# A four-layer graph network on one Trainium2 core: zero-filled operands, projections read together, halves with banks of their own, and some one-hot rows built by ScalarE

## The chip, the cores and the metric

The kernel runs on one core of a Trainium2 chip. The core has a matrix engine (TensorE, PE in the profile, with its weight loads as PEld), a vector engine (VectorE, DVE), an activation engine (ScalarE, ACT), a general engine (GpSimd, POOL) and a queue engine (SyncE, SP). Data lies in SBUF with 128 partitions; TensorE writes to PSUM, which has eight banks of 128 x 512 fp32 each. The metric is device time in microseconds for one launch.

## The reference

There are 32 graphs (batches) of 512 nodes with 128 features and a 0/1 adjacency matrix. Each of four layers normalizes x, clips it at zero, computes an update and adds it to x.

```python
h = jnp.maximum(_layernorm(x, axis=-1), 0.0)
x = x + _L0_gnn_ref(h, adj, L0_gnn_W, L0_gnn_b)   # max over neighbours of relu(p_i + q_j + b)
h = jnp.maximum(_layernorm(x, axis=-1), 0.0)
x = x + _L1_gnn_ref(h, adj, ...)                  # four dense layers over both directions of adj
h = jnp.maximum(_layernorm(x, axis=-1), 0.0)
x = x + _L2_gnn_ref(h, adj, L2_gnn_weight, L2_gnn_bias)   # row-normalized adj @ (h @ W) + b
h = jnp.maximum(_layernorm(x, axis=-1), 0.0)
x = x + _L3_gnn_ref(h, adj, nodemask, ...)        # four rounds of message and GRU cell
...
# layer 0
p = jnp.einsum('bnd,do->bno', x, W1 - W2)
q = jnp.einsum('bnd,do->bno', x, W2)
pre = p[:, :, None, :] + q[:, None, :, :] + b
h = jax.nn.relu(pre) * adj[..., None]
return jnp.max(h, axis=2)
# one of the four layers inside layer 1
src_agg = jnp.einsum('bjv,bij->biv', src, _l2norm(adj, 2))
dst_agg = jnp.einsum('bjv,bji->biv', dst, _l2norm(adj, 1))
upd = jnp.concatenate([src_agg, self_rep, dst_agg], axis=2)
return jnp.tanh(upd @ wu + bu)
# one of the four rounds of layer 3
m = jnp.einsum('bjn,bjd->bnd', adj, hw)
h = _gru_cell(m, h, w_ih[i], w_hh[i], b_ih[i], b_hh[i])
```

## The kernel before

A batch of 512 nodes is handled as NT = 4 tiles of 128 nodes. The function `batch` chains four stages for one batch.

`prepare` normalizes x, makes the adjacency matrix and its transpose (`at`) in SBUF, computes q and p of layer 0 by TensorE (`pq`), and writes the table of q to DRAM. It counts, by a triangular matmul (`pc`), which neighbour in its half block of 64 nodes each neighbour is; ScalarE copies the counts to `cc`, and SyncE copies these to both halves of the partitions (`ccd`). It forms keys by matmul (`pkey`), takes the eight largest by VectorE (`top`) for the neighbours beyond four in a half block, and transposes a small table of degree factors `sc` (`psc`).

`gathers` computes the maximum over neighbours. For each source block jt and each slot k from 1 to 4, VectorE compares `ccd` with 64 + k, which gives one-hot rows `oh` of 128 x 1024. Two matmuls with the split values of q (`qhl`) pick the q of the k-th neighbour (`pa`), and VectorE keeps the running maximum in `acc`. Up to seven leftover neighbours are fetched by indirect DMA on GpSimd's queue into `G` and joined into `gm`.

`layer1` runs four dense layers. A layer transposes its input (`pf`), splits it into a high part (ScalarE) and a low part (VectorE), and multiplies both by `at` and by `an`, sixteen matmuls into two banks `pg`, with VectorE scaling each bank into `ag`. It then sums in the bank `pu`: a bias matmul of `b8` with `rows` (8 partitions deep), and the products of the earlier features and of `ag` with fused weights. ScalarE takes the tanh of the bank. `layer23` does layer 2 (one aggregate, four 128-column projections `po`, each added to x by VectorE) and the four GRU rounds of layer 3 (`pk`, `pg3`, `phn`, `pxn`, `ph`). In the last batch alone the GRU rounds run by halves of 256 nodes; both halves of `ph` lie in one bank, and so do the two products `phn` and `pxn` of a half.

Nothing of this is issued in the order in which it is written. Every call is noted in a `Flow` (line 285), which issues all instructions by a list scheduler: it holds up to AHEAD = 6 batches open, estimates each instruction's cost, and gives the engine that can start first the waiting instruction with the earliest due time. A due time is a batch's place times PACE less the length of what follows less a lead that depends on the stage (`LEADS`). `FIRST`, `LAST` and `WEIGHTS` shift the places of the first and last batches and of the weight preparation. `BANKS` says how many PSUM banks each of four users is guaranteed: ps0 (prepare), ps1 (layer 1), ps2 (layers 2 and 3) and ps3 (the `pa`); the rest of the eight is shared. The scheduler knows a dependency only through the view that an instruction names: `mm` and `tr` take a view of the bank that they write, and `mm` may name the whole bank instead by `group`. Where TensorE would stand idle for long, the scheduler inserts idle-time matmuls (`spin`).

```python
F.mm(po[:, t, :], mT[:, t, :], W.w2, start=True, stop=True)
F.mm(flat(pu), W.b8[:, i, :], rows, start=True, stop=False)
F.vec.tensor_scalar(oh, ccd[jt], NBASE + k, None, ALU.is_equal)
op.due = n * self.pace - op.due - op.lead
```

All recorded instructions carry line 510, where the scheduler issues them, so the profile is read by tile names. Weights are prepared in `FastWeights` (`first`, `rest`, `last`) in the same flow.

Of the kernel before, what the change touches and what calls it, by code (L numbers as in the profile page):

```python
# [32 lines left out]
CODES = ((0, 1), (P, 1), (2 * P, 2), (4 * P, 4))  # L33
NLEFT = 7
PACE = 45.35
SPACING = 1.8
AHEAD = 6
BANKS = (2, 1, 2, 1)

LEADS = {  # L40
    "prepare": -33.2, "counts": -28.6, "keys": -38.2, "rows": -9.6,
    "gather0": 12.6, "gather1": -3.5, "gather2": -1.7, "gather3": -10.5,
    "first": 14.4, "layer1": -15.5, "layer10": -39.2, "layer11": -39.2,
    "layer12": -26.1, "layer13": -57.9, "layer2": 50.7, "layer3": 187.5,
    "layer30": 155.2, "layer31": 193.8, "layer32": 81.5, "layer33": 66.2,
    "out": 33.8,
}
FIRST = (-0.01, -0.0, -0.31, 0.0)
LAST = (0.0, -0.23, -0.17, -0.97, -0.05)
WEIGHTS = (-5.87, -1.69, -2.33)  # L50
# [205 lines left out]
class Engine:  # L256
# [5 lines left out]
    def __getattr__(self, op):  # L262
        fn = getattr(self.real, op)

        def note(*args, **kw):
# [12 lines left out]
            fast = self.name == "vec" and op == "tensor_scalar" and outs[0].free_size() > 256  # L278
# [6 lines left out]
class Flow:  # L285
# [50 lines left out]
    def cost(self, engine, op, outs, ins):  # L336
# [4 lines left out]
        if "dma" in op:  # L341
            if engine != "pool":
                width = 2 if outs[0].dtype == BF16 else 4
                return 0.48 if engine == "sync" else 0.42, 2.0 + outs[0].size() * width / 1.2e5
            return (1.25, 6.0) if "indirect" in op else (0.7, 4.0)
# [52 lines left out]
    def mm(self, out, lhsT, rhs, start, stop, group=None):  # L398

        n = rhs.free_size()  # L400
# [9 lines left out]
    def tr(self, out, in_, ident):  # L410
        self.note(
            "pe", self.nc.tensor.transpose, (out, in_, ident), {}, [out], [in_, ident],
            0.109 if in_.dtype == F32 else 0.056, 0.16,
        )
# [189 lines left out]
class FastWeights:  # L604
# [5 lines left out]
    def __init__(self, nc, F, a, const, mid, ps):  # L610
# [47 lines left out]
        nc.gpsimd.memset(self.sign[0:4, 1:2], 0.0)  # L658
        self.nc, self.a, self.const, self.n = nc, a, const, n

    def own(self, shape, dtype, name):
        return self.F.tile(self.const, shape, dtype, name, name)

# [28 lines left out]
    def rest(self):  # L692
# [31 lines left out]
        self.b8 = self.own([8, NL1, P], F32R, "b8r")  # L724
# [6 lines left out]
        for i in range(NL1):  # L731
# [4 lines left out]
            for k, nm in enumerate(("ws", "wn", "wd")):  # L736
# [8 lines left out]
                F.vec.tensor_copy(wt, pt[:, 0:ch, :])  # L745
# [10 lines left out]
            for k in range(2):  # L756
# [11 lines left out]
                self.b8[:, i, :], hi.bitcast(F32), self.sign[0:8, 0:1], full, ALU.mult, ALU.add  # L768
            )

    def last(self):
# [14 lines left out]
        F.vec.tensor_copy(w3t, pt[:, 0:NL3, :])  # L786
        self.gh, self.gm = [], []
        for l in range(NL3):
            for nm, dst in (("hh", self.gh), ("ih", self.gm)):
# [9 lines left out]
                if nm == "hh":  # L799
                    F.vec.tensor_copy(t, pg[:, 0:3, :])  # L800
                else:
                    gt = self.temp("xn2", f"gt_{l}")[:, 0:3, :]
                    F.vec.tensor_copy(gt, pg[:, 0:3, :])
# [19 lines left out]
def fast(ctx: ExitStack, tc: tile.TileContext, a: dict, out: bass.AP, bad):  # L823
# [12 lines left out]
    F.share(ps, 8, {f"ps{s}": n for s, n in enumerate(BANKS)} | {"idle": 0})  # L836

# [58 lines left out]
    def transposed(s, src, name):  # L896

        pt = pst(s, name)
        for t in range(NT):
            F.tr(pt[:, t, :], src[:, t, :], W.ident)  # L900
        return pt
# [9 lines left out]
    def parts(s, src, tag, buf=plain, cuts=(slice(None),)):  # L911
# [3 lines left out]
        for c in cuts:  # L915
            v, h, l = ((w if len(cuts) == 1 else w[:, c, :]) for w in (src, hi, lo))
            F.act.copy(h, v)
            F.vec.tensor_sub(l, v, h.bitcast(F32))
        return hi, lo

    def aggregate(s, two, m, name):

        pg = pst(s, name)
        hi, lo = two
        for jt in range(NT):
            F.mm(flat(pg), hi[:, jt, :], m[:, jt, :], start=(jt == 0), stop=False)
            F.mm(flat(pg), lo[:, jt, :], m[:, jt, :], start=False, stop=(jt == NT - 1))
# [3 lines left out]
    def prepare(b, xt, af):  # L931
# [64 lines left out]
        F.lead = LEADS["counts"]  # L996
# [16 lines left out]
        F.lead = LEADS["keys"]  # L1013
# [4 lines left out]
        sc = F.tile(small, [P, 6, NT], F32, tag="sc", name=f"sc_{b}", bufs=4)  # L1018
# [36 lines left out]
        F.tr(pt[0 : 6 * NT, 0, :], sc.rearrange("p k t -> p (k t)"), W.ident)  # L1055
# [7 lines left out]
    def gathers(b, at, ccd, qhl, pn, tab, idx, has, dinv):  # L1063
# [15 lines left out]
        for jt in range(NT):  # L1079
            F.lead = LEADS[f"gather{jt}"]  # L1080
            for k in range(1, KSLOT + 1):
                oh = F.tile(big, [P, 2, N], F32R, tag="oh", name=f"oh_{b}_{jt}_{k}", bufs=3)
                F.vec.tensor_scalar(oh, ccd[jt], NBASE + k, None, ALU.is_equal)
# [7 lines left out]
        F.lead = LEADS["first"]  # L1091
# [16 lines left out]
    def layer1(b, x1, an, at, dinv):  # L1108
# [6 lines left out]
        rows = F.tile(mid, [8, N], F32R, tag="rows", name=f"rows_{b}")  # L1115
# [3 lines left out]
        F.act.copy(rows, row8)  # L1119
# [3 lines left out]
        feat = {"h": hT}  # L1123
        agg = {}
        new = "h"
        for i in range(NL1):
            F.lead = LEADS[f"layer1{i}"]
            names = INPUTS[i]
            w = W.w1[i]
            if i:  # L1130

                pt = transposed(1, feat[new], f"pf_{b}_{i}")
                two = parts(1, pt, f"{b}_1_{i}")
            ag = F.tile(mid, [P, 2, N], F32, tag="ag" + {"f2": "f1"}.get(new, new), name=f"ag_{b}_{i}")
            for k, m in ((0, at), (1, an)):
                pg = aggregate(1, two, m, f"pg_{b}_{i}_{k}")
                F.vec.tensor_mul(ag[:, k, :], flat(pg), rbc[:, k, :])
            agg[new] = ag
            pu = pst(1, f"pu_{b}_{i}")
            F.mm(flat(pu), W.b8[:, i, :], rows, start=True, stop=False)  # L1140
            late = []
            for c, nm in enumerate(names):
                F.mm(flat(pu), w[:, 1, c, :], flat(feat[nm]), start=False, stop=False)
                for k in range(2):
                    if nm == new:
                        late.append((c, k))
                        continue
                    F.mm(flat(pu), w[:, 2 * k, c, :], agg[nm][:, k, :], start=False, stop=False)
            for c, k in late:
                F.mm(flat(pu), w[:, 2 * k, c, :], ag[:, k, :], start=False, stop=(k == 1))  # L1150
# [3 lines left out]
            F.act.activation(fi, pu, AF.Tanh, bias=W.bu[:, i : i + 1])  # L1154
            feat[new] = fi
        F.lead = LEADS["layer2"]
# [613 lines left out]
```

## Time and profile before

| | us |
|---|---|
| median of 3 runs | 2941.53 |
| lowest and highest | 2940.82, 2942.3 |
| the profiled execution | 2943.54 |
| its span, first to last instruction | 2941.8 |
| TensorE busy | 2843.4 |
| VectorE busy | 2384.2 |
| GpSimd busy | 1827.3 |
| ScalarE busy | 1218.1 |

The mean granted TensorE clock is 0.993 of full speed. In the profile, a group's row gives the line, engine, operation, what is written from what is read with partitions x elements, the count, the time in which the engine was busy with it, the mean duration of one in ns, and the idle time of the engine just before such instructions with what ended it. A fp32 matmul stands as two records. The ends of matmuls are modelled and overlap, so the distance between starts is what one of them takes from TensorE. The row of tenths shows 40 slices of the span.

### The profile page before, as it was taken

Reading aid. Unit: us, or ns where it says so; the run is one execution under the profiler, and the core shown is the slowest. Engines: PE = TensorE matmul, PEld = TensorE weight load, DVE = VectorE, ACT = ScalarE, POOL = GpSimd, SP = SyncE. Lnnn points to the kernel's source line nnn. Section 1 sums busy time; section 2 is a strip of 40 time slices with the busy share of each in tenths; the row PEclk is TensorE's granted clock in tenths of the full one; section 3 lists DMA queues with packets and bytes.
Section 4 is the critical chain, followed back from the end, with each engine's and each line's share of the span. In section 5 each row is a group of like instructions: output and inputs, shape, how many; then the busy total and the mean of one; then the engine's idle time right before and its main releaser. Section 6 shows DMA issues by size and latency. Waiting matters only on the chain.

```text
span 2941.8 us, 37748 instructions
## 1 busy us (share of the span) xinstructions
PE 2843.4 (97%) x11493; PEld 1753.8 (60%) x11513; DVE 2384.2 (81%) x5382; ACT 1218.1 (41%) x2547; POOL 1827.3 (62%) x2013
## 2 busy tenths in 40 slices
PE   7899999999999999999999999999999999999997
PEld 3555556666666566666666566666666666555555
DVE  6988878888888898888888888889888888887533
ACT  2434434434444344344444444444344444333323
POOL 4676667666666666666666666666666666565312
PEclk8999999999999999999999999999999999999999
DMA  7642434334334334333433433343333333342100
GB/s 154 145 91 48 84 69 86 85 72 81 65 66 86 85 74 86 59 72 80 86 85 73 84 61 65 86 87 77 80 68 69 75 86 84 56 77 37 33 4 9
DMA packets 191267, 218.44 MB, mean 74 GB/s; under 512 B 30376, under 2 KB 139600, under 8 KB 191056
## 3 DMA queue, kind: packets, MB, share of 16 engines
q0 software_dynamic: 47104, 92.34, 22.2%
q1 hardware_dynamic: 73768, 63.63, 7.4%
q10 hardware_dynamic: 70184, 59.98, 6.7%
q8 instruction: 93, 1.52, 0.2%
q14 instruction: 118, 0.97, 0.1%
HBM read 164.32 MB, written 17.96 MB: 62 GB/s over the span
## 4 chain that ended last, share of the span: by engine, by line
PE 80%; DVE 10%; issue 4%; DMA 2%; ACT 2%; POOL 1%; ACTq 0%; SPq 0%; DVEq 0%; POOLq 0%
PE pg L510 25%; PE pu L510 19%; PE pk L510 15%; PE pa L510 6%; PE phn L510 4%; PE pxn L510 3%; DVE acc L510 3%; PE pkey L510 2%; PE ph L510 2%; PE pf L510 2%; PE po L510 1%; DMA G<-qtab,idx 1%; DVE nn L510 1%; PE pt L510 1%; DVE x L510 1%
## 5 line engine op out<-in xcount | busy, mean ns | idle before, releaser
L510 POOL DMA_INDIRECT G<-qtab,idx x768 | 848.6, 1105 | 589.6 <-DVE gm L510 453.3
L510 DVE TENSOR_TENSOR acc<-acc,pa 128x512 f32<-128x512 f32 x992 | 673.6, 679 | 146.4 <-PE pa L510 134.5
L510 PE MATMUL pa<-oh,qhl 128*128 128x512 f32 x1024 | 465.7, 510 | 11.2 <-DVE oh L510 5.3
L510 PE MATMUL pg<-an,hi 128*128 128x512 f32 (+1 forms) x1040 | 457.3, 441 | 0.6 <-DVE acc L510 0.4
L510 PE MATMUL pu<-ag,w 128*128 128x512 f32 x896 | 448.0, 592 | 0.5 <-DVE ag L510 0.3
L510 PE MATMUL pg<-an,lo 128*128 128x512 f32 (+1 forms) x1040 | 436.0, 422 | 0.0
L510 DVE TENSOR_SCALAR oh<-ccd 128x1024 fp32r<-128x1024 bf16 x512 | 393.9, 787 | 13.3 <-PE pa L510 13.2
L510 PE MATMUL pg<-at,lo 128*128 128x512 f32 x640 | 295.9, 462 | 0.8 <-DVE lo L510 0.4
L510 PE MATMUL pg<-at,hi 128*128 128x512 f32 x640 | 281.1, 439 | 7.2 <-DVE acc L510 1.8
L510 PEld LDWEIGHTS pa<-oh,qhl 128*128 128x128 f32 x1024 | 193.9, 191 | 152.2 <-issue 40.4
L510 ACT ACTIVATE xn<-x,shift,rstd 128x128 f32<-128x128 f32 x512 | 211.5, 484 | 171.6 <-POOL shift L510 170.1
L510 DVE TENSOR_TENSOR gm<-gm,G 128x128 f32<-128x128 f32 x768 | 253.4, 331 | 8.7 <-DMA G<-qtab,idx 7.7
L510 PE MATMUL pk<-h,g_hh 128*128 128x512 f32 (+1 forms) x528 | 256.3, 590 | 0.6 <-DVE top L510 0.6
L510 PEld LDWEIGHTS pg<-an,hi 128*128 128x128 f32 x1040 | 195.1, 188 | 93.2 <-issue 49.1
L510 PEld LDWEIGHTS pg<-an,lo 128*128 128x128 f32 x1040 | 195.2, 188 | 84.7 <-issue 40.3
L510 PE MATMUL pk<-mT,g_ih 128*128 128x512 f32 (+1 forms) x528 | 242.3, 580 | 1.4 <-ACT mT L510 1.1
L510 ACT ACTIVATE gate<-pk,bsum 128x512 f32<-128x512 f32 (+1 forms) x264 | 176.9, 673 | 140.8 <-PE pk L510 137.3
L510 PEld LDWEIGHTS pu<-ag,w 128*128 128x128 f32 x896 | 168.1, 189 | 110.9 <-issue 80.0
L510 POOL TENSOR_TENSOR rstd<-rstd,mhalf 128x4 f32<-128x4 f32 x128 | 139.8, 1092 | 138.8 <-DVE shift L510 133.6
L510 DVE TENSOR_TENSOR ag<-pg,rbc 128x512 f32<-128x512 f32 x256 | 174.8, 684 | 61.3 <-PE pg L510 58.5
L510 ACT COPY mT<-pg 128x512 f32<-128x512 f32 (+1 forms) x164 | 94.2, 575 | 304.6 <-PE pg L510 300.0
L510 ACT CAST hi<-ph 128x512 fp32r<-128x512 f32 (+1 forms) x99 | 56.8, 574 | 341.2 <-PE ph L510 333.4
(172 smaller groups left out, 5110.4 us busy)
## 6 DMA issues: line engine op xcount, KB each, us to landing
af<-in_adj_dram ACTq DMA_DIRECT2D x32, 1024.0 KB
ccd<-cc SPq DMA_DIRECT2D x512, 64.0 KB
an<-in_adj_dram POOLq DMA_DIRECT2D x128, 256.0 KB, 3.9
x<-in_x_dram ACTq DMA_DIRECT2D x64, 256.0 KB
rbc<-scal SPq DMA_DIRECT2D x32, 512.0 KB
G<-qtab,idx POOLq DMA_INDIRECT x768, 3.8
qtab<-qn SPq DMA_DIRECT2D x128, 64.0 KB
out_dram<-xo ACTq DMA_DIRECT2D x32, 256.0 KB
```

Source lines behind the costliest of these rows:

```text
L510: op.fn(*(real(v) for v in op.args), **{k: real(v) for k, v in op.kw.items()})
```

## The change

The diff does the following.

- `b8` and `rows` become full 128-partition operands that are filled with zeros once, in the new function `zeros`; only eight partitions carry values. `sc` becomes part of one of two fixed 128 x 128 tiles with zeros (`vectors`), and its transposition takes all of it.
- The four `po` products name the whole bank as what they write, and so do the transposes.
- In the last batch's GRU rounds, the two halves of `ph` get a bank each, and `phn` and `pxn` of a half are issued one after the other ahead of the reads.
- `layer1` of batches 0 and 31 runs by halves of 256 nodes: each half has its own banks for the transposed input, for `pg` and for `pu`.
- In batch 0, 1 and 2, ScalarE builds 2, 2 and 1 of the four slots' one-hot rows, in two passes: the absolute distance from 64 + k, and then relu of one less that distance.
- ScalarE instead of VectorE copies the transposed weights.
- The planner's numbers are others: PACE, SPACING, LEADS, FIRST, LAST, WEIGHTS, the kept banks (ps0 1 instead of 2, ps1 2 instead of 1), leads of their own for the first and the last batch, and the estimated cost of an indirect DMA.

```diff
+ONACT = (2, 2, 1, 0)
 NLEFT = 7
-PACE = 45.35
-SPACING = 1.8
+PACE = 46.14
+SPACING = 1.5
 AHEAD = 6
-BANKS = (2, 1, 2, 1)
+BANKS = (1, 2, 2, 1)
...
+FIRST = (1.57, 0.36, -0.05, 0.0)
+LAST = (0.0, 0.18, 0.33, 0.24, 0.3)
+WEIGHTS = (-3.98, -2.44, -5.94)
...
-            fast = self.name == "vec" and op == "tensor_scalar" and outs[0].free_size() > 256
+            fast = self.name == "vec" and op == "tensor_scalar"
...
-            return (1.25, 6.0) if "indirect" in op else (0.7, 4.0)
+            return (1.05, 6.0) if "indirect" in op else (0.7, 4.0)
...
-    def tr(self, out, in_, ident):
+    def tr(self, out, in_, ident, group=None):
         self.note(
-            "pe", self.nc.tensor.transpose, (out, in_, ident), {}, [out], [in_, ident],
+            "pe", self.nc.tensor.transpose, (out, in_, ident), {}, [group or out], [in_, ident],
...
+        self.rows = self.zeros([P, n // P, P], "rows")
+        self.vectors = []
+        for i in range(2):
+            t = fixed([P, P], F32, f"vectors{i}")
+            nc.gpsimd.memset(t, 0.0)
+            self.vectors.append(F.fixed(t, [P, P], F32))
...
+    def zeros(self, shape, name):
+        t = self.const.tile(shape, F32R, name=name)
+        for k in range(shape[1]):
+            self.nc.vector.tensor_scalar(t[:, k, :], self.ident, 0.0, None, ALU.mult)
+        return self.F.fixed(t, shape, F32R)
...
-        self.b8 = self.own([8, NL1, P], F32R, "b8r")
+        self.b8 = self.zeros([P, NL1, P], "b8r")
...
-                F.vec.tensor_copy(wt, pt[:, 0:ch, :])
+                F.act.copy(wt, pt[:, 0:ch, :])
...
-        F.tr(pt[0 : 6 * NT, 0, :], sc.rearrange("p k t -> p (k t)"), W.ident)
+        F.tr(pt[:, 0, :], full, W.ident)
...
-                F.vec.tensor_scalar(oh, ccd[jt], NBASE + k, None, ALU.is_equal)
+                if k > KSLOT - ONACT[min(b, len(ONACT) - 1)]:
+
+                    far = F.tile(big, [P, 2, N], BF16, tag="far", name=f"far_{b}_{jt}_{k}")
+                    F.act.activation(far, ccd[jt], AF.Abs, bias=W.slot[:, k : k + 1])
+                    F.act.activation(oh, far, AF.Relu, bias=W.ones[:, 0:1], scale=-1.0)
+                else:
+                    F.vec.tensor_scalar(oh, ccd[jt], NBASE + k, None, ALU.is_equal)
...
+        step = NT // 2 if b in (0, B - 1) else NT
+        cuts = [slice(t, t + step) for t in range(0, NT, step)]
+        cols = [slice(c.start * P, c.stop * P) for c in cuts]
...
-            pu = pst(1, f"pu_{b}_{i}")
-            F.mm(flat(pu), W.b8[:, i, :], rows, start=True, stop=False)
+            pus = [pst(1, f"pu_{b}_{i}_{j}") for j in range(len(cuts))]
+            pus = [cut(pu, slice(0, step)) for pu in pus]
+            for pu, c in zip(pus, cols):
+                F.mm(flat(pu), W.b8[:, i, :], flat(W.rows)[:, c], start=True, stop=False)
...
-            F.mm(po[:, t, :], mT[:, t, :], W.w2, start=True, stop=True)
+            F.mm(po[:, t, :], mT[:, t, :], W.w2, start=True, stop=True, group=po)
...
-            pt = pst(s, f"ph_{b}_{l}")
-            for c, (vh, vx) in zip(cuts, halves):
-                F.mm(flat(vh), W.gh[l][:, 2, :], flat(cut(h, c)), start=True, stop=True)
+            pts = [pst(s, f"ph_{b}_{l}_{c.start}") for c in cuts]
+            for c, (vh, vx), bank_, pt in zip(cuts, halves, phn, pts):
+                bank_ = bank_ if len(cuts) > 1 else None
+                F.mm(
+                    flat(vh), W.gh[l][:, 2, :], flat(cut(h, c)), start=True, stop=True, group=bank_
+                )
+                F.mm(
+                    flat(vx), W.gm[l][:, 2, :], flat(cut(mT, c)), start=True, stop=True, group=bank_
+                )
                 F.vec.scalar_tensor_tensor(
                     cut(nn, c), vh, W.bhh[:, n : n + 1], cut(r, c), ALU.add, ALU.mult
                 )
-                F.mm(flat(vx), W.gm[l][:, 2, :], flat(cut(mT, c)), start=True, stop=True)
```

## What the change does to the time: the prediction

> **What bounds the kernel now.** I read the page first, then busy time by stretches, then the groups of instructions with their shapes kept apart, then the timeline of TensorE around two places that the diff touches. All times are of the profiled execution: its span is 2941.8 us, its own time 2943.54 us, and the median of the runs shown is 2941.53 us, 2.0 us less.
>
> ```profile
> span 2941.8 us, 37748 instructions
> PE 2843.4 (97%) x11493; PEld 1753.8 (60%) x11513; DVE 2384.2 (81%) x5382; ACT 1218.1 (41%) x2547; POOL 1827.3 (62%) x2013
> PE   7899999999999999999999999999999999999997
> DVE  6988878888888898888888888889888888887533
> PEclk8999999999999999999999999999999999999999
> ```
>
> TensorE is busy nearly everywhere, but "busy" overlaps pipelined matmuls and hides small losses, so I count its work by the distance from one start to the next. In the timeline that distance is 0.23 us for a 512-column fp32r matmul, 0.43 for each of the two records of a 512-column fp32 matmul, 0.215 for 256 columns of the latter, 0.11 for a fp32 transpose or a record of po, 0.056 for a 128-column bf16 one. Per batch, by the counts of the groups divided by 32: 104 pg, 32 pa and 4 pc at 0.23 (32.2 us); 90 fp32 records of pu, pk, phn and pxn (38.6); 8 of pq (1.7); 8 of po (0.9); 48 transposes (5.2); 48 bf16 (2.7); the four bias matmuls at 0.51 (2.0); psc 0.2. That is 83.5 us. The result stores of the middle are 86.7 us apart (989.9 to 2463.3 us for 17 batches). So in the middle TensorE has 96% of every batch filled with work, and what shortens a batch must shorten TensorE's own stream.
>
> The ends differ:
>
> ```profile
> core 0: us, PE busy (x) PEld busy (x) DVE busy (x) ACT busy (x) POOL busy (x), PEclk, DMA share, GB/s
> 0.00:50.00 50.00, 32.96 (x168) 17.63 (x170) 25.16 (x66) 16.84 (x52) 19.61 (x41) 0.96 0.69 187
> 50.00:100.00 50.00, 42.02 (x205) 22.85 (x206) 46.23 (x112) 15.06 (x41) 34.62 (x42) 0.84 0.84 137
> 100.00:150.00 50.00, 42.74 (x198) 26.55 (x199) 47.08 (x111) 21.71 (x50) 32.46 (x37) 0.93 0.57 123
> 150.00:200.00 50.00, 46.88 (x175) 28.13 (x177) 45.85 (x110) 15.67 (x38) 36.96 (x37) 0.97 0.46 91
> 1200.00:2000.00 800.00, 792.79 (x3216) 493.96 (x3215) 682.26 (x1527) 347.60 (x719) 522.48 (x571) 1.00 0.37 76
> 2850.00:2900.00 50.00, 46.88 (x189) 29.20 (x190) 21.23 (x55) 19.27 (x37) 14.21 (x17) 1.00 0.00 0
> 2900.00:2941.80 41.80, 27.72 (x144) 20.36 (x145) 14.41 (x35) 11.45 (x28) 6.92 (x12) 0.90 0.05 15
> ```
>
> From 50 to 200 us VectorE is busy 139 of 150 us and ScalarE about a third. There TensorE's counted work is only 20, 33 and 40 of each 50 us, some of it at a clock of 0.84 to 0.97. The last 90 us hold 60 us of work: one batch's chain is left, with waits.
>
> **The change, part by part.** *The bias operand (b8, rows) with 128 rows.* The timeline of TensorE and of its weight loads around one such matmul:
>
> ```profile
> 1004.41 0.40 PE L510 MATMUL pg<-an,lo 128*128 128x512 f32 x1
> 1004.64 0.39 PE L510 MATMUL pg<-at,hi 128*128 128x512 f32 x1
> 1004.96 0.49 PE L510 MATMUL pu<-rows,b8r 8*128 8x512 f32 x1
> 1005.38 0.50 PE L510 MATMUL pg<-an,hi 128*128 128x512 f32 x1
> 1004.96 0.18 PEld L510 LDWEIGHTS pu<-rows,b8r 8*128 8x128 f32 x1 [0.36 <-issue]
> 1005.38 0.19 PEld L510 LDWEIGHTS pg<-an,hi 128*128 128x128 f32 x1 [0.24 <-issue]
> ```
>
> Neighbours start 0.23 apart; the 8-row one starts 0.32 after its predecessor and its successor 0.42 after it. Neither weight load begins before its matmul, while elsewhere the load runs ahead. The same 0.32 and 0.42 are the medians over the middle. The pair takes 0.74 instead of 0.46: 0.28 us, four times a batch. The Trainium skill (TensorE: Matmul & The Clock Gate, Why this matters for your kernels, row on small K) says the reverse of a gain here: one matmul of K=32 takes as long as one of K=128. By that rule this part is worth 0. I take the row, because the rule is of one matmul alone and the trace shows the neighbours paying. 128 x 0.275 = 35 us; batch 0's lie where TensorE isn't the limit, so 33. Ends: 0 and 35.
> The fills are 8 small VectorE operations of about 0.28 us (the row of code<-ident has that) = 2.2 us and a few memsets on GpSimd. VectorE is idle from 6.4 to 17.1 us, waiting for low, which covers the fills; without cover they cost 2.2 us.
> *psc with 128 columns.* After psc the next matmul starts at 0.225 instead of 0.11, but its weight load waits for ScalarE's h there, and once, ahead of a transpose, it was 0.11. Ends 0 and 3.7 us; I take 1.
> *Projections po issued together.*
>
> ```profile
> 1001.58 0.83 PE L510 MATMUL po<-w,mT 128*128 128x128 f32 x6
> 1002.93 0.49 PE L510 MATMUL po<-w,mT 128*128 128x128 f32 x2 [0.51 <-DVE x L510]
> 1003.17 0.47 PE L510 MATMUL pg<-at,lo 128*128 128x512 f32 x1
> ```
>
> The fourth product waits until VectorE has read the first out of the same bank: the planner had put that read before it. From third to fourth the starts lie 0.79 apart instead of 0.11, 31 times. With the whole bank as the group, all four stand ahead of every read. 31 x 0.67 = 21 us, 19 where TensorE is the limit. VectorE's first read comes some 0.2 us later; x3's norm follows, far ahead of its use in the middle.
> *One-hot rows by ScalarE in batches 0, 1, 2 (8, 8, 4 of 16), weight copies by ScalarE.* One row of these carries VectorE's part, from its groups in 50 to 200 us:
>
> ```profile
> L510 DVE TENSOR_SCALAR oh<-ccd 128x1024 fp32r<-128x1024 bf16 x41 | 30.4, 750 | 0.3 <-PE pa L510 0.2
> ```
>
> VectorE loses 20 x 0.79 = 15.7 us of oh and 9.6 us of copies (wt, w3t, g_hh, gt: 1.7+1.6+1.2+0.7+2.2+2.2), 25 us in all. ScalarE has no row of this shape: its copies of 256, 384 and 512 columns took 373, 480 and 587 ns, so 1024 would be about 1.02 us, and Abs plus Relu 2.1 (an estimate from these). It gains 42 us of one-hots and some 9 of copies in 250 us, and goes from 35% to about 57%. The Trainium skill (ScalarE: Activation LUTs, Rules for kernel authors) sends relu to VectorE, as faster per element; by its measure the move is a loss of 2.1 against 0.79. I take the stage: VectorE is 93% busy there, and per source block 8.6 us of VectorE (4 oh, 8 maxima of 0.68) become 7.0 beside 4.2 of ScalarE. Batch 0's pa run from 37.6 to 72.7 us, 35.1, just what 4 x 8.6 makes. So 6.3 us each for batches 0 and 1, half of 3.1 for batch 2 (TensorE is 80% filled by then), a third of the copies: 17, less 2 for what queues behind the long activations on ScalarE (xn, cc, hi, whose readers are VectorE and TensorE). I take 15; ends -5 (ScalarE late) and 25.
> *Halves.* In layer 1 of batches 0 and 31, 256-column fp32r matmuls started 0.12 apart in layer 3 of the last batch, so a pair costs 0.238 against 0.231: +0.5 us a batch on TensorE, +1.7 on VectorE, +1.5 on ScalarE, beside TensorE's other work. What it buys is a chain with shorter waits. Own banks in the last batch: its second-half transposes waited for VectorE or ScalarE reading the first half (0.5, 0.5 and 0.7 us at 2908.2, 2919.3, 2930.0), about 3 us over the layers. Layer 1 by halves and the last batches' earlier places act on idle time: 2750 to 2941.8 holds about 152 us of work, so 39 idle. I take 5 for these, 8 with the banks; ends 0 and 18.
> *Leads, places, gaps, kept banks.* These reorder every engine's list. The middle's remaining idle is 3.2 us a batch, of which 0.67 is po. A new order can move it either way; I take 0, with 0.5 us a batch to both sides (14 us). The gathers' gap falls from 1.8 to 1.5 in the planner alone; POOL is 62% busy.
>
> Sum: 33 + 1 + 19 + 15 + 8 = 76. 2943.5 - 76 = 2867.5; less the 2.0 between this execution and the median, 2865 us. The middle's batch would be 86.7 - 1.1 - 0.7 = 84.9 us. VectorE's 74 us a batch (682 of 800) are then 87%: next in line, not yet the limit.
>
> **The rivals.** *The rule is right:* 128 rows cost what 8 did, and the gaps have another cause, such as the first matmul of a group. Then 33 us stay: 2898. Against it, the first matmuls of other groups (pk<-h) start on the beat.
> *VectorE or ScalarE gives nothing back at the ends,* or VectorE's 87% makes new waits in the middle: without start and tail 23 us are gone, 2888. For it: DVE acc waited for PE 134.5 us in total, a sign of lists that must mesh.
> *Slower: ps0's guarantee falls from two banks to one.* Counts and keys fill four banks pc and four pkey per batch; a bank is free again after ScalarE's cc (0.58) or VectorE's maximum (0.69). If TensorE stood for each, 4 x 0.58 + 4 x 0.69 = 5.1 us a batch over 29 batches, +148: 3013 us. It decides from 2.6 us a batch, half of these evictions uncovered. For it: TensorE takes its list in order, so all behind it waits. Against: the sum of kept banks stays 6 of 8, two can be borrowed, and TensorE waited for top only 0.6 us in all.
>
> **How the numbers follow.** Likeliest case, 2840 to 2890: 0.68. The rule right, 2898: 0.09. No gain at the ends, 2888: 0.12. A better order in the middle too, 2830 to 2840: 0.05. Banks or another wait, over 2936: 0.06. The range takes in the full start gain and half a microsecond a batch below (2865 - 10 - 14 - 9 = 2832) and the rule's case above with a little ill luck (2903). About 0.2% (5.9 us) is what a measurement can tell from no change: faster 0.93, same 0.02, slower 0.05.
>
> **What would show it.** Right: the row of pu<-rows,b8r has the form 128*128 and starts 0.23 from both neighbours; po x8 without a wait; stores 84.9 us apart; TensorE's busy share higher in 50 to 200 us, VectorE's oh x492; no more table loads than the three of 1.28 us now. Wrong: b8r still at 0.32 and 0.42; waits of PE for ACT oh in the first 200 us; PE waiting for ACT cc or DVE top in every batch; stores over 86 us apart.

## The result and the profile after

The changed kernel takes 2905.4 us (median of 4 runs, 2903.9 to 2910.69), the kernel before 2941.18 us: a ratio of 0.9884 [0.9866, 0.9901]. That is 36 us less where 76 were forecast; the time lies 2.4 us above the predicted range. The profiled execution took 2910.69 us, its span is 2909.0. The kernel before was timed anew with each group of runs, with medians from 2939.6 to 2948.1 us, so runs of different groups are compared by their ratios to it.

First the page of the changed kernel, its span, its busy times and two rows of tenths.

```profile
span 2909.0 us, 38588 instructions
PE 2795.8 (96%) x11766; PEld 1794.6 (62%) x11766; DVE 2299.1 (79%) x5371; ACT 1268.4 (44%) x2622; POOL 1848.5 (64%) x2020
PE   7799999999999999999999999999999999999998
PEclk9999999999999999999999999999999999999999
```

TensorE's busy time fell by 48 us and VectorE's by 85, but the span by only 33. Counted by distances between starts, as in the prediction, TensorE's work fell by an estimated 39 us, from 2684 to 2645: the operands gave what they should. The rest of the span, idle-time matmuls included, rose from 258 to 264.

Then the timeline of TensorE and its weight loads at the two places that the prediction showed.

```profile
1002.63 1.11 PE L529 MATMUL po<-w,mT 128*128 128x128 f32 x8
1003.50 0.49 PE L529 MATMUL pg<-at,hi 128*128 128x512 f32 x1
1003.82 0.39 PE L529 MATMUL pg<-an,hi 128*128 128x512 f32 x1
1004.05 0.39 PE L529 MATMUL pu<-rows,b8r 128*128 128x512 f32 x1
1004.27 0.59 PE L529 MATMUL pu<-f,w 128*128 128x512 f32 x1
...
1038.86 0.19 PEld L529 LDWEIGHTS pu<-rows,b8r 128*128 128x128 f32 x1
1039.09 0.39 PE L529 MATMUL pu<-rows,b8r 128*128 128x512 f32 x1
```

The bias matmul has the form 128*128 and starts 0.23 after its predecessor; its successor starts 0.22 after it. For the one at 1039.09 the weight load runs 0.23 ahead, as it did not at the place shown of before. The `po` stand together, x8, without a wait.

The busy times by stretches of the changed kernel:

```profile
core 0: us, PE busy (x) PEld busy (x) DVE busy (x) ACT busy (x) POOL busy (x), PEclk, DMA share, GB/s
0.00:50.00 50.00, 34.25 (x172) 18.95 (x172) 24.70 (x72) 24.02 (x61) 13.53 (x47) 0.93 0.62 179
50.00:100.00 50.00, 36.19 (x205) 24.28 (x206) 35.16 (x80) 33.33 (x65) 30.14 (x36) 0.91 0.80 141
100.00:150.00 50.00, 41.55 (x240) 29.47 (x241) 43.04 (x110) 38.02 (x80) 37.57 (x43) 0.98 0.57 113
150.00:200.00 50.00, 46.26 (x238) 36.58 (x236) 37.83 (x113) 21.75 (x42) 32.32 (x33) 0.94 0.41 77
1200.00:2000.00 800.00, 783.54 (x3225) 497.12 (x3224) 661.81 (x1540) 345.48 (x716) 535.41 (x570) 1.00 0.38 76
```

In the start VectorE fell from 139 to 116 us of the 150 between 50 and 200, and ScalarE rose from 52 to 93, as the split says. TensorE is no busier there. In the middle its share fell from 99 to 98%: it waits where it did not before.

The starts of the result stores tell where the time went. Head, middle and tail are cut at the ninth store (out 8) and the 26th (out 25):

| us | before | after | difference |
|---|---|---|---|
| start to out 8 | 989.9 | 995.1 | +5.2 |
| out 8 to out 25, 17 batches | 1473.4 | 1473.0 | -0.4 |
| out 25 to the end | 478.5 | 440.9 | -37.6 |
| one batch in the middle | 86.67 | 86.65 | 0.0 |

So nothing came from where the prediction had put most of it, and all of it from the tail, for which only a part of 8 us was forecast. The wait that ate most of the middle's gain is in the list of TensorE's waits from 400 to 2500 us, changed kernel:

```profile
engine line waited for: us in total, times, longest us
PE pg L529 <- DVE lo L529: 21.1, 24, 0.9
PE spin L553 <- DVE lo L529: 8.7, 24, 0.4
PE pg L529 <- ACT hi L529: 5.5, 24, 0.2
```

The same list of the kernel before had `po` as its only large row, and no wait for `lo` among its rows:

```profile
PE po L510 <- DVE x L510: 12.3, 24, 0.5
PE pu L510 <- ACT rows L510: 2.9, 4, 1.1
PE ph L510 <- DVE h L510: 0.8, 2, 0.4
```

One large wait went, and three came, once in each of 24 batches. The largest is that of `pg` for `lo`, which VectorE writes. One such place in the timeline of the changed kernel (start, duration, engine, operation, output from input):

```profile
1072.17 1.33 POOL L529 TENSOR_TENSOR gate<-h,gate 128x512 f32<-128x512 f32 x1
...
1072.34 1.32 DVE L529 TENSOR_TENSOR gm<-gm,G 128x128 f32<-128x128 f32 x1
...
1073.58 1.46 DVE L529 TENSOR_TENSOR acc<-acc,pa 128x512 f32<-128x512 f32 x2
...
1074.31 0.49 PE L529 MATMUL pg<-an,hi 128*128 128x512 f32 x1
1074.96 0.68 DVE L529 TENSOR_TENSOR lo<-pf,hi 128x512 fp32r<-128x512 f32 x1
...
1075.70 0.50 PE L529 MATMUL pg<-at,lo 128*128 128x512 f32 x1 [0.90 <-DVE lo L529]
```

The join `gm` starts 0.17 us after GpSimd's gate product and takes 1.32 us, where most take 0.28. It ends 0.16 after the gate does. Behind it in VectorE's list stand two maxima and then the `lo` for which TensorE waits. The next start should be 0.23 after 1074.31 and comes 1.39 after it: 1.16 us lost, in a batch whose bound is TensorE.

The wait for `hi`, 0.23 us each, stands just ahead of this place. That of `spin` belongs to a second place, where the planner has put three idle-time matmuls:

```profile
1031.61 0.81 PE L553 MATMUL spin<-code,identb 128*128 128x512 bf16 x3 [0.36 <-DVE lo L529]
1032.57 0.47 PE L529 MATMUL pg<-an,hi 128*128 128x512 f32 x1
```

From the wait ahead of them to the next `pg` these are 1.3 us a batch without work. The changed kernel has such a place in each of the 17 batches of the middle, the kernel before has none there.

### The profile page after: what moved, and what is told of

Read it like the earlier page. It is cut to its first block, busy times and chain, and to the rows that moved or that the text cites. A ratio compares the mean times of both kernels' runs of the same rounds, so it can differ in the third digit from the quotient of the medians.

```text
span 2909.0 us, 38588 instructions
## 1 busy us (share of the span) xinstructions
PE 2795.8 (96%) x11766; PEld 1794.6 (62%) x11766; DVE 2299.1 (79%) x5371; ACT 1268.4 (44%) x2622; POOL 1848.5 (64%) x2020
## 4 chain that ended last, share of the span: by engine, by line
PE 85%; DVE 7%; DMA 2%; issue 2%; ACT 2%; POOL 1%; SPq 0%; ACTq 0%; DVEq 0%; POOLq 0%
PE pg L529 26%; PE pu L529 19%; PE pk L529 14%; PE pa L529 7%; PE phn L529 4%; PE pxn L529 4%; DVE acc L529 3%; PE ph L529 2%; PE pq L529 2%; PE pkey L529 2%; PE pt L529 1%; DVE lo L529 1%; PE pf L529 1%; PE po L529 1%; PE px L529 1%
## 5 line engine op out<-in xcount | busy, mean ns | idle before, releaser
L529 PE MATMUL pg<-an,lo 128*128 128x512 f32 (+1 forms) x1072 | 461.9, 433 | 0.0
L529 PE MATMUL pa<-oh,qhl 128*128 128x512 f32 x1024 | 450.5, 508 | 6.1 <-DVE acc L529 2.1
L529 PE MATMUL pu<-ag,w 128*128 128x512 f32 (+1 forms) x952 | 448.0, 568 | 4.1 <-DVE ag L529 4.1
L529 DVE TENSOR_SCALAR oh<-ccd 128x1024 fp32r<-128x1024 bf16 x492 | 348.9, 723 | 62.4 <-PE pa L529 55.0
L529 PE MATMUL pg<-at,lo 128*128 128x512 f32 (+1 forms) x672 | 295.9, 442 | 22.8 <-DVE lo L529 22.3
L529 PE MATMUL pg<-at,hi 128*128 128x512 f32 (+1 forms) x672 | 272.7, 407 | 8.4 <-ACT hi L529 7.2
L529 DVE TENSOR_TENSOR gm<-gm,G 128x128 f32<-128x128 f32 x768 | 242.4, 322 | 3.5 <-DMA G<-qtab,idx 3.3
L529 DVE TENSOR_TENSOR ag<-pg,rbc 128x512 f32<-128x512 f32 (+1 forms) x272 | 172.5, 653 | 71.5 <-PE pg L529 69.7
L529 DVE SCALAR_TENSOR_TENSOR nn<-phn,bcol,gate 128x512 f32<-128x512 f32 (+1 forms) x132 | 96.3, 729 | 148.2 <-ACT gate L529 148.1
L529 POOL TENSOR_TENSOR rstd<-rstd,mhalf 128x4 f32<-128x4 f32 x128 | 152.7, 1193 | 86.9 <-DVE shift L529 82.6
```

What stands on the lines that cost most here:

```text
L529: op.fn(*(real(v) for v in op.args), **{k: real(v) for k, v in op.kw.items()})
```

## The experiments

**The operands, without any new order.** `e1_pad` is the kernel before with only the 128-row `b8` and `rows` (one `rows` for all batches instead of one each); `e2_po` is the kernel before with the late `po` put ahead of the first read of its bank in the finished order; `e3_pad_po` does both. Everything else stands in the lists as before.

```diff
-        self.b8 = self.own([8, NL1, P], F32R, "b8r")
+        self.b8 = self.zeros([P, NL1, P], "b8r")
...
-            F.mm(flat(pu), W.b8[:, i, :], rows, start=True, stop=False)
+            F.mm(flat(pu), W.b8[:, i, :], flat(W.rows), start=True, stop=False)
```

```diff
+        if kind == "op" and x.engine == "pe" and isinstance(x.args[0], View):
+            k = name_of(x.args[0])
+            if k.startswith("po_") and n > first[k]:
+                moved.setdefault(first[k], []).append(n)
+                skip.add(n)
```

> The kernel before with one edit: the bias operands b8 and rows are 128 partitions deep, filled with zeros; every engine's list stays in the order it had. Theory L (the lists: an operand edit is worth what the prediction said, and the changed kernel lost it again by the new order of its lists): 33 us faster, about 2908; stores of the middle 85.6 us apart; b8r starts 0.23 from both neighbours. Theory B (something other than TensorE sets the middle, VectorE or GpSimd): within 8 us of before, stores still 86.5 to 86.7 apart. Theory R (small K costs nothing, as the skill's rule has it): within 5 us of before and the gaps around b8r remain.

> The kernel before with one edit: the fourth po product of a batch is issued ahead of VectorE's first read of that bank; each engine's own list stays in its order. Theory L: the wait of 0.67 us goes 31 times, 19 us faster, about 2922, stores 86.0 apart. Theory B: another wait takes its place, less than 5 us.

> Both edits of the operands and of po in the lists of before. Theory L: they add up, 52 us faster, about 2889 and so faster than the changed kernel; stores 84.9 apart. Theory B: 2925 or more; the middle doesn't fall below 86 us a batch.

Measured: `e1_pad` 2919.91 us, 0.9899 [0.9883, 0.9914]; `e2_po` 2924.83 us, 0.992 [0.9906, 0.9933]; `e3_pad_po` 2897.34 us, 0.9821 [0.9808, 0.9834]. That is 28, 23 and 51 us, and the stores of the middle lie 86.0, 86.0 and 85.2 us apart. The two edits add up. They beat the whole change.

**The operands taken out of the changed kernel.** `e4_after_8row` has the changed kernel's lists and 8-row operands.

```diff
-        self.rows = self.zeros([P, n // P, P], "rows")
+        self.rows = F.fixed(fixed([8, n // P, P], F32R, "rows"), [8, n // P, P], F32R)
...
-        self.b8 = self.zeros([P, NL1, P], "b8r")
+        self.b8 = self.own([8, NL1, P], F32R, "b8r")
```

> The changed kernel with b8 and rows 8 partitions deep again, its lists in the same order. Theory L: TensorE's stream is still part of what sets a batch, but it now stands for VectorE's lo once a batch, so some of the 35 us that come back hide in that wait: 15 to 35 us slower than the changed kernel, 2920 to 2940. Theory B: less than 5 us slower, 2905 to 2910.

Measured: 2947.05 us, 0.9997 [0.999, 1.0003], some 33 us above the changed kernel, stores 87.8 us apart, 1.1 a batch more. The 128 rows gain there too; so the rest of the change lost in the middle what they gained.

**The tail.** `e6_after_last_old` has the changed kernel with `LAST` of before; `e7_after_whole` runs layer 1 of the last batch whole.

```diff
-LAST = (0.0, 0.18, 0.33, 0.24, 0.3)
+LAST = (0.0, -0.23, -0.17, -0.97, -0.05)
```

```diff
-        step = NT // 2 if b in (0, B - 1) else NT
+        step = NT // 2 if b in (0,) else NT
```

> The changed kernel with LAST alone as before (the places of the last three batches later again), the lists the same until these batches come up. If the gain at the end comes from the places in the order: 30 to 50 us slower than the changed kernel, about 2945 by the times so far, ratio about 1.00 to before, and the last store again 30 us or more after the one before it. If it comes from the halves and their banks: within 10 us of the changed kernel.

> The changed kernel with layer 1 of the last batch whole instead of by halves, lists the same until that batch comes up. If the places make the gain at the end: within 6 us of the changed kernel (ratio 0.987 to 0.991). If the halves make it: 20 us or more slower.

Measured: `e6_after_last_old` 2946.52 us, 0.9997 [0.9988, 1.0006], its last two stores 72 us apart (2864.7 and 2936.4) instead of 1.1; `e7_after_whole` 2912.91 us, 0.9884 [0.9867, 0.99], the ratio of the changed kernel. So without the new places of the last batches the tail's gain is gone, and the halves of layer 1 in the last batch give nothing that shows: from out 25 to the end the profiled executions have 443.9 us without them and 440.9 with them, and the intervals are wider than this.

**The start.** `e5_onact_held` is `e3_pad_po` in which ScalarE builds the one-hot rows of the first three batches and copies the weights, each at the place in the order that VectorE's had. `e8_less_oh` is `e3_pad_po` in which those 20 one-hot operations aren't computed at all: it leaves out these neighbours of layer 0, and `pa` reads the rows of a slot one or two below.

```diff
+            far = self.far(n)
+            self.nc.scalar.activation(far, real(x.args[1]), AF.Abs, bias=self.slot[:, k : k + 1])
+            self.nc.scalar.activation(
+                real(x.args[0]), far, AF.Relu, bias=self.one[:, 0:1], scale=-1.0
+            )
+            return True
```

```diff
+            if kind == "op" and x.engine == "vec" and x.args and isinstance(x.args[0], View):
+                if self.left_out(name_of(x.args[0])):
+                    continue
```

> The kernel with both operand edits in the lists of before (e3_pad_po), and in it the start's relief alone: in batches 0, 1 and 2 ScalarE builds 2, 2 and 1 of the four slots' one-hot rows and ScalarE copies the transposed weights, each at the place in the order where VectorE's operation stood. The prediction's step (VectorE sets the start, its 25 us are worth 15): 15 us faster than e3_pad_po, a ratio of about 0.977 to before, stores of the first eight batches 15 us earlier. Rival (the start is a chain from load through ScalarE, GpSimd and VectorE to TensorE, in which the longer passes of ScalarE stand too): within 5 us of e3_pad_po, ratio 0.981 to 0.984.

> The kernel with both operand edits in the lists of before (e3_pad_po) with VectorE's load in the start taken away and given to nobody: the 20 one-hot rows of batches 0, 1 and 2 that the change moves to ScalarE are not computed (pa reads those of the slot two, or one, below, so layer 0 of these three batches lacks these neighbours). If VectorE's busy time sets the start: at least 12 of the 15.7 us come back, ratio about 0.978 to before, stores from the first on 12 us earlier than in e3_pad_po. If the start is a chain in which VectorE is busy but not the only link: less than 6 us, ratio 0.980 to 0.983.

Measured: `e5_onact_held` 2907.1 us, 0.9867 [0.9851, 0.9884], some 13 us above `e3_pad_po`; VectorE's busy time from 0 to 250 us fell from 201.0 to 177.1 and out 8 still left 9.6 us later. `e8_less_oh` 2893.06 us, 0.9819 [0.9803, 0.9835], the same as `e3_pad_po`. Its trace shows where the relief went. By the first store TensorE is 6.1 us ahead of `e3_pad_po` (283.5 against 289.6). Near 300 us it loses 2.5 of these, after a wait of 1.9 us for ScalarE's `h`, and near 375 us the rest: `pu` waits 4.0 us instead of 2.3 for `rows`, which ScalarE copies when a DMA has landed. Beside both, the granted clock was 0.83 (300 to 310 us) and 0.82 (380 to 390), where `e3_pad_po` had 1.00. The third store leaves 0.1 us later. So in those lists relieving VectorE, even for free, buys 6 us in the start, half of the 12 expected if VectorE sets it, and nothing in the end. The stretch from 50 to 150 us, first of `e5_onact_held`:

```profile
core 0: us, PE busy (x) PEld busy (x) DVE busy (x) ACT busy (x) POOL busy (x), PEclk, DMA share, GB/s
50.00:100.00 50.00, 37.66 (x190) 22.40 (x193) 36.30 (x90) 31.36 (x62) 31.71 (x39) 0.84 0.88 147
100.00:150.00 50.00, 39.19 (x181) 25.13 (x181) 34.43 (x86) 34.86 (x65) 28.79 (x35) 0.85 0.45 93
```

and of `e3_pad_po`:

```profile
50.00:100.00 50.00, 40.01 (x196) 22.54 (x199) 44.98 (x110) 15.26 (x41) 34.58 (x42) 0.84 0.77 120
100.00:150.00 50.00, 42.15 (x194) 26.59 (x196) 46.85 (x111) 20.60 (x48) 33.63 (x39) 0.93 0.63 136
```

With the split all of TensorE, VectorE and GpSimd do less in this stretch, and the clock granted from 100 to 150 us is 0.85 instead of 0.93. The two ScalarE passes are longer than the operation that they replace, and they stand in VectorE's places; of TensorE's matmuls `pa` and their weight loads, the waits for ScalarE's `oh` came to 8.4 and 11.2 us in the first 200 us. Of the 6.7 us that `e5_onact_held` is behind at the first store, by the distances between starts an estimated 5 are longer waits of TensorE and 2 slower matmuls.

**The new wait.** `e9_after_swap` tries to part gate and `gm` on GpSimd's side: in 25 batches the gate product goes behind the adjacency load that follows it.

```diff
+        if names[a].startswith("an_") and names[b].startswith("gate1_") and names[c].startswith("an_"):
...
+                acts.insert(c, acts.pop(b))
```

> The changed kernel with one place in GpSimd's list exchanged in 25 batches: the multiplication gate<-h,gate of the last GRU round goes behind the adjacency load that follows it. In the changed kernel that multiplication starts just ahead of VectorE's gm, which then takes 1.3 us instead of 0.28, and TensorE stands 1.16 us for VectorE's lo soon after. If this meeting on the two engines' shared access makes the wait: gm 0.28, the wait nearly gone, 15 to 27 us faster than the changed kernel, stores 85.5 us apart, ratio about 0.981. If the wait only moves on (another link of the same loop stands): less than 6 us, ratio 0.987 to 0.990.

Measured: 2939.88 us, 0.9985 [0.9977, 0.9993], some 30 us above the changed kernel, a miss. The timeline of `e9_after_swap` at one such place:

```profile
1075.97 1.13 POOL L606 DMA_DIRECT2D an<-in_adj_dram  x2
...
1076.72 1.83 DVE L606 TENSOR_TENSOR gm<-gm,G 128x128 f32<-128x128 f32 x1
...
1077.10 1.29 POOL L606 TENSOR_TENSOR gate<-h,gate 128x512 f32<-128x512 f32 x1
```

The later gate didn't let `gm` through. This `gm` starts 0.38 us before the gate, while GpSimd issues the load, stays through the whole gate, and ends 0.16 after it: 1.83 us instead of 1.32. TensorE waited for `lo` as before (21.2 us in 24 waits from 400 to 2500 us), and for `acc` besides (12.2 us in 23).

`e10_after_gm` moves the other one. In the 24 batches, VectorE's `gm` goes from two maxima ahead of `lo` to right behind it; all other lists stay.

```diff
+        kinds = [names[i + j].split("_")[0] for j in range(4)]
+        if kinds != ["gm", "acc", "acc", "lo"] or names[i + 3].split("_")[2] != "1":
+            continue
+        a, d = vec[i], vec[i + 3]
...
+        acts.insert(d, acts.pop(a))
```

`e11_after_numbers` has the changed kernel's code with other leads, places and paces in the planner, so the same instructions in other lists.

```diff
-PACE = 46.14
-SPACING = 1.5
+PACE = 46.22060016239077
+SPACING = 1.5031415956246768
```

> The changed kernel with one instruction of VectorE moved in 24 batches: the product gm, which in the trace of the changed kernel starts 0.2 us after GpSimd's 128x512 gate product and takes 1.30 to 1.34 us instead of 0.28, goes behind the lo copy of layer 1 that TensorE waits for. All other lists are the same. If the long gm is what makes lo late, lo comes about 1 us earlier in each of these batches, most of the 1.16 us wait of the gate matmuls goes, and the kernel gains 15 to 27 us on the changed one: ratio to before about 0.981, stores about 85.5 us apart. If lo is late for another reason, or the wait only moves to the next thing that VectorE delivers (as the swap on GpSimd's list did), less than 6 us: 0.986 to 0.991, stores 86.2 to 86.7 apart.

> The changed kernel's code with other numbers in its planner (costs and leads), so that the same instructions stand in other lists; nothing else. If what the changed kernel has lost in the middle against the operand edits alone lies in the order of its lists, other lists move the time: about 10 to 15 us below the changed kernel, ratio to before about 0.984, stores about 85.9 us apart. If it lies in the code (halves, banks, the split one-hot rows) or in another bound, the time stays within 4 us of the changed kernel: 0.987 to 0.990, stores 86.5 or more apart.

Measured: `e10_after_gm` 2882.49 us, 0.9799 [0.9783, 0.9816], 23 us below the changed kernel by the medians, 25 by the ratios; stores 85.4 apart in most batches, 85.56 in the mean. Its timeline at the place shown above:

```profile
1062.57 2.27 DVE L617 TENSOR_TENSOR acc<-acc,pa 128x512 f32<-128x512 f32 x3 [0.39 <-PE pa L617]
1063.00 1.33 POOL L617 TENSOR_TENSOR gate<-h,gate 128x512 f32<-128x512 f32 x1
...
1064.76 0.68 DVE L617 TENSOR_TENSOR lo<-pf,hi 128x512 fp32r<-128x512 f32 x1
1064.98 0.40 PE L617 MATMUL pg<-an,hi 128*128 128x512 f32 x1
...
1065.36 0.28 DVE L617 TENSOR_TENSOR gm<-gm,G 128x128 f32<-128x128 f32 x1
...
1065.49 0.50 PE L617 MATMUL pg<-at,lo 128*128 128x512 f32 x1
```

The gate takes 1.33 us as before, but now three maxima stand beside it. Each of them reads one operand from PSUM, and they go on at 0.76 us each. `gm` takes 0.28 once more. `lo` starts 1.76 us after the gate instead of 2.79. The 1.16 us at this place are down to 0.28; the wait of `pg` for `lo` is gone from the list of waits. The place with the three idle-time matmuls is still there, 1.3 us a batch.

`e11_after_numbers`: 2941.11 us, 1.0005 [0.9996, 1.0014]. I had expected 10 to 15 us below the changed kernel; it is some 35 above. That the order moves the time is shown, its direction I had wrong. Its waits from 400 to 2500 us:

```profile
PE pg L508 <- DVE lo L508: 28.5, 38, 1.3
PE ph L508 <- DVE h L508: 10.9, 22, 1.1
```

**The split inside the lists that were planned for it.** `e12_gm_oh_back` is `e10_after_gm` with the one-hot rows and weight copies of the start back on VectorE, each at its place.

```diff
+        if n.startswith("oh_"):
+            k = int(n.split("_")[3])
+            self.nc.vector.tensor_scalar(
+                real(x.args[0]), real(self.ccd), NBASE + k, None, ALU.is_equal
+            )
+            return True
```

> The kernel with the moved gm (ratio 0.980), and in it the 20 one-hot operations of batches 0 to 2 and the weight copies that the change gave to ScalarE go back to VectorE, each at its place in the order; TensorE's, GpSimd's and SyncE's lists are the same. This undoes the start's part inside the changed kernel. If that part costs time as it did in the old lists (13 us), this kernel is 8 to 14 us faster: ratio 0.975 to 0.977, and out#8 leaves at about 975. If the new lists, which were planned with the split, gain from it as the prediction had it (15 us), it is 10 to 16 us slower: about 0.985. If the start is bound by something else (matmuls at a low clock, the chain through each batch), within 4 us: 0.979 to 0.981.

Measured: 2895.05 us, 0.9826 [0.9813, 0.984], 8 us above `e10_after_gm` by the ratios and 13.6 by the spans of the profiled executions (2895.0 and 2881.4). The first store leaves 13.0 us later (291.1 against 278.1), and the distance holds to the end. Here the split gains. How much of the 13.0 us is VectorE's load is open: by the distances between starts, an estimated 4 are longer waits of TensorE, 2 idle-time matmuls and 7 slower matmuls. The clock granted in the four stretches of 50 us from 0 to 200 was 0.86, 0.88, 0.85 and 0.93, against 0.93, 0.88, 0.98 and 0.97 in `e10_after_gm`, and no run parts the clock from the waits.

## Why the prediction fell short

**The bias operand** (33 us): right. 28 us in the old lists, 33 in the new ones, and 0.23 us from start to start. By the row on small K of the Trainium skill (TensorE: Matmul & The Clock Gate, Why this matters for your kernels), which is of one matmul alone, this part would be worth nothing; for a matmul that stands between 128-row ones `e1_pad` shows otherwise.

**The projections** (19 us): right; 23 us alone, and 51 for both against 52 predicted. psc (1 us) did shorten: the next matmul starts 0.108 us after it instead of 0.225; its share of the time wasn't measured.

**The start** (15 us): the step was that VectorE's 93% sets the time there. It held in part at most: 15.7 us of VectorE's work taken away gave 6 in the start and none in the end (`e8_less_oh`). In the lists of before the split costs 13 us (`e5_onact_held`); in those planned with it, taking it back costs 8 to 14 (`e12_gm_oh_back`). That this lies near the 15 is luck: without the split the new lists have out 8 at 999.3, 23 us behind `e3_pad_po`, and the split gives back 13 of a loss that the new order made. The advice of the Trainium skill (ScalarE: Activation LUTs, Rules for kernel authors) that sends relu to VectorE was right for the old lists and wrong for the new ones. Two prices were a little off. A `oh` on VectorE was taken at 0.79 us, the mean of the whole execution; the row shown for 50 to 200 us has 0.75. A ScalarE pass takes 1.15 us where 1.02 to 1.05 were estimated, as these two rows of the changed kernel from 0 to 200 us have it.

```profile
L529 ACT ACTIVATE far<-ccd,slot 128x1024 bf16<-128x1024 bf16 x20 | 23.0, 1150 | 3.6 <-DMA ccd<-cc 3.5
L529 ACT ACTIVATE oh<-far,ones 128x1024 fp32r<-128x1024 bf16 x20 | 23.0, 1150 | 1.5 <-PE pa L529 1.5
```

**Halves and banks** (8 us): layer 1's halves in the last batch give nothing that shows (`e7_after_whole`). The halves of batch 0 and the banks of the GRU rounds weren't tried alone. The tail's 37.6 us hang on the places of the last batches: with `LAST` of before they are lost (`e6_after_last_old`). I had put these places under the same few microseconds.

**Leads, places, gaps, kept banks** (0, with 0.5 us a batch to both sides): this is the step that failed. The new lists cost the middle 1.45 us a batch against `e3_pad_po`, which has the same operands in the old lists (86.65 against 85.2), three times what I had allowed. 1.09 of it is one instruction in VectorE's list (`e10_after_gm`, 85.56). The remaining 0.36 a batch is not settled; the three idle-time matmuls with the waits around them, 1.3 us a batch in both of these kernels, have no counterpart in the middle of `e3_pad_po`, and no run took them out. The head has not gained what the operands alone give it there (out 8 at 995.1, with `e3_pad_po` at 976.1). 9 of these 19 us come back with the moved `gm` (986.1). The other 10 are the 23 that the new order still loses there, less the 13 of the split (`e12_gm_oh_back`); where the 23 arise is open. Against this the tail gained 29 us more than in `e3_pad_po` (440.9 against 469.7). In sum, what the change does beyond the operands and `po` was forecast to gain 24 us (1 + 15 + 8); against `e3_pad_po` it cost 15 by the spans of the profiled executions (2909.0 against 2894.2) and 18 by the ratios.

None of my rivals had this wait. The one of the banks did not come: the list of waits of the changed kernel has neither `cc` nor `top`. VectorE's load I had as a rival, by its share of the middle; what it came to was one instruction of VectorE at the wrong place. The printed kernel even has a term for it: `port` in the planner keeps operations of VectorE and GpSimd apart that have two operands in SBUF (a line of the diff, `fast`, changes its condition), but by estimated times, and at the place shown the two started 0.17 us apart. The means hid it: in the pages `gm` has a mean of 331 ns in the kernel before, 322 in the changed one and 292 in `e10_after_gm`. The view by tile has minimum, median and maximum; from 500 to 2400 us in the kernel before

```profile
L510 DVE TENSOR_TENSOR gm<-gm,G x528: 255/281/1599, 500.5 to 2392.7; 128x128 f32<-128x128 f32 x176
```

and in `e10_after_gm`

```profile
L617 DVE TENSOR_TENSOR gm<-gm,G x531: 268/281/893, 507.0 to 2393.6; 128x128 f32<-128x128 f32 x177
```

Over the whole execution 31 of 768 took more than 0.9 us in the kernel before, 28 in the changed one and 5 in `e10_after_gm`. So the long `gm` was there to be seen: at 1069.40 us, 1.56 us beside a gate of 1.30 at 1069.51. There it cost TensorE no wait that the list shows: two maxima and `nn` stood behind it, and no `lo` that TensorE lacked.

The Trainium skill (SBUF — State Buffer, SBUF: two separate sides) states a reason: a VectorE operation with two SBUF inputs and a GpSimd operation that reads SBUF exclude each other for the length of the whole instruction. The trace agrees: `gm`, with both inputs in SBUF, ended 0.16 us after the gate in the changed kernel and in `e9_after_swap`, and the maxima, with one input in PSUM, ran on. Over the whole changed kernel the medians beside a gate are 1.32 us for `gm` (26 times, 0.28 over all), 1.18 for `nn<-nn,zc`, which also has both inputs in SBUF (35 times, 0.68 over all), and for the maxima 0.68, as over all (135 times). By the page the one that starts first has its way; in `e9_after_swap` the profile has `gm` held though it starts 0.38 us ahead of the gate. The profile's spans on GpSimd are rough, so which came first stays open. The issue of a DMA alone is not the cause: beside a gather's issue without a gate, `gm` took a median of 0.28 us in the kernel before (157 times). With that rule beside the maximum of this row, a prediction could have put an estimate on a reordering: up to 1.3 us wherever such a join comes to stand ahead of what TensorE waits for, in 24 batches up to 31 us. `e10_after_gm` got 23 to 25 of such a loss back.

Best of all kernels here is `e10_after_gm` with 0.9799 [0.9783, 0.9816]; `e3_pad_po`, two edits without any new plan, has 0.9821 [0.9808, 0.9834], and the intervals overlap.

## What to carry to other kernels

Where a planner reorders everything, an edit's own gain and the new order's cost are two terms of the same size: measure the edit in the old lists first, and give the order a range from the worst stall that the trace already shows. Read the maximum of a group, not only its mean, and ask what stands behind the long ones in their engine's list. Whether moving work between engines pays is not a property of the work: the same move cost 13 us in one order and gained 8 to 14 in another.

## What I had not expected of the hardware

- A VectorE operation of 0.28 us with both inputs in SBUF was held for 1.32 us by GpSimd's 128x512 product, until 0.16 us after its end; where the profile has it start 0.38 us ahead of that product, it took 1.83 us. Maxima with one input in PSUM weren't held (0.68 us at 135 such places).
- An 8-row operand between 128-row ones costs its neighbours time: four a batch made 0.8 us of each batch in one order (86.0 of `e2_po` against 85.2 of `e3_pad_po`) and 1.1 in another (87.8 of `e4_after_8row` against 86.65).
- ScalarE's Abs and Relu passes over 128x1024 bf16 took 1.15 us each, in the old lists (`e5_onact_held`) and in the new ones.
